# ScalarE writes the first terms of two PSUM accumulations, and one VectorE step finishes each output bank

## The chip, the cores and the metric

One Trainium2 chip, one core of it. The metric is device time in microseconds, from the first to the last instruction of one launch with what lies around it; the kernel's time is the median of its runs. Lower is better. All data are float32 (the adjacency is int32).

## The reference, cut to what matters

`x` is 16 x 512 x 512 (batch, node, feature), one condition vector of 512 per batch, an adjacency with 11 labels, 20 key nodes, 16 heads of 32, and two directions `d`. Biases of the projections are small random numbers.

```python
row_zero = exp_v.sum(-1) == 0
q_exp = jnp.where(row_zero[..., None], 0.0, q[:, None, :])
vcq = jnp.concatenate([exp_v, q_exp], axis=-1)
self_feat = vcq @ W_self.T + b_self
output = self_feat
for d in range(2):
    A = adj_f if d == 0 else jnp.swapaxes(adj_f, 1, 2)
    A = A[:, :, :NONGT, :]
    cond = A.sum(-1)
    vb = A @ w_bias + b_bias
    output = output + _gat_attention(self_feat, cond, vb, Wq[d], bq[d], Wk[d], bk[d], Wout[d], bout[d])
rel = jax.nn.relu(output)
return exp_v + rel
```

`_gat_attention` takes queries from all 512 nodes and keys and values from the first 20, masks scores where `cond` is zero, adds `vb`, takes the softmax over the 20 keys and multiplies by the values and `Wout`.

## The kernel before, in words

Everything is held transposed: feature on the 128 partitions in four chunks, node along the free axis. A setup stage folds `Wq` and the keys into one matrix `g` per batch and `Wout` and the values into `vd`, so that the loop over the 16 batches has three kinds of matmul. Each is issued in pieces of 32 output partitions, four of which run side by side.

**self_feat (`product`, L251).** The product of `x` with half of the weights is done as a 2 x 2 block product with seven block products instead of eight (Strassen's scheme in Winograd's form). `x_sum` (L234, GpSimd) forms the sums of `x` blocks; `weight_sums` did so once for the weights. Products 1, 6, 7 and 4 accumulate in this order in `ps_a` (two banks, one for each half of the rows), and the running sum is read between them; product 2 goes to `ps_d`; products 5 and 3 accumulate in `ps_c`. The term of the condition vector is rank one: the flag row `nz` (is the row of `x` non-zero) times a column `qw`. `partial` (L286, VectorE) adds it while it moves `ps_a` into a block of `sf`, in two instructions; `joined` (L298, VectorE) adds `ps_d` or `ps_c` to a block. `block(b, f, l)` is half `f` of the features by half `l` of the nodes. The first 20 nodes come from the setup by `new_self` (ScalarE).

**scores (L350).** 128 nodes a tile (`nt` 0 to 3), both directions and all heads, into `ps_s`. Then, for each tile: `weigh` (VectorE) adds the mask and bias table `full` (L380), takes the maximum (L384) and subtracts it (L388), `expo` (ScalarE, L393), `normal` (VectorE sum L416 and reciprocal L417, GpSimd multiplication L418) and `turn` (VectorE transposition, L425).

**attend (L427).** For a whole batch: weights times `vd`, 24 matmuls into the four banks `ps_o`, with `start` on the first round. `finish` (L442) adds `sf` (VectorE, L445) and takes bias and ReLU (ScalarE, L447); `residual` (GpSimd, L450) adds `x`; `store` sends the rows on SP's queue.

**masks.** `mask_mul` (ScalarE, 11 instructions, L318) multiplies labels by `w_bias`; `mask_count` (VectorE L323, GpSimd L324) counts edges; `mask_sum` (VectorE, L329) sums; `mask_spread` (ScalarE, 32-partition copies, L338) lays the sum out for the heads; `full_add` (GpSimd, L345) makes `full`. `row_sum` (ScalarE, L193) makes the row sums of `x` two batches ahead.

The order on each engine is the order of the program text; there is no scheduler. Batches overlap: in iteration `b`, tile 0 has product 4, half of the scores, the other half, and product 3, all of batch `b`; tile 1 has scores; tile 2 has the attend block of batch `b-1`, scores, and products 1 and 2 of batch `b+1`; tile 3 has product 6, scores, products 7 and 5 of `b+1`. So on TensorE one batch reads: 4, scores 0, 3, scores 1, attend, scores 2, 1, 2, 6, scores 3, 7, 5. PSUM has two double banks for `ps_s` and four single banks that `ps_a` (0 and 1), `ps_d` (2), `ps_c` (3) and `ps_o` (0 to 3) take in turn. Loads wait in SP's queue, each behind a named instruction (`done[...]`).

Of the kernel before, what the change touches and what calls it, by code (L numbers as in the profile page):

```python
# [13 lines left out]
P = 128  # L14
# [4 lines left out]
def gat_kernel(  # L19
# [55 lines left out]
    qw = const.tile([P, C, B], F32, name="qw")  # L75
    bo = const.tile([P, C], F32, name="bo")
# [174 lines left out]
    def product(b, n):  # L251
# [11 lines left out]
        if n == 1:  # L263
            parts[b, "a"] = [bank(f"ps_a{b}_{i}", i if b else None) for i in range(2)]
        if n == 2:
            parts[b, "d"] = bank(f"ps_d{b}", 2 if b else None)
        if n == 5:
            parts[b, "c"] = bank(f"ps_c{b}", 3 if b else None)
        for i in range(2):
            for k in range(2):  # L270
                for a in range(HL):
# [12 lines left out]
                    nc.tensor.matmul(to, lhs, x[:, k], start=start, stop=stop, skip_group_check=n != 2)  # L284

    def partial(b, f, l):  # L286

        to = block(b, f, l)
        for i in range(2):
# [3 lines left out]
            )  # L293

# [132 lines left out]
    def attend(b, banks, tiles=slice(0, NT), start=True, stop=True):  # L427
# [4 lines left out]
        for first, runs in ((True, ((1, 2, 1), (5, 2, 3))), (False, ((0, 1, 0), (3, 1, 2), (4, 1, 2), (7, 1, 4)))):  # L432
            for at, n, j in runs:
                for a in range(HL):
# [4 lines left out]
                        start=start and first, stop=stop and not first,  # L439
                    )  # L440

    def finish(b, o, banks):  # L442

        for c in range(C):
            done["add", c] = nc.vector.tensor_add(o[:, c], banks[c], sfs[b][:, c])  # L445
        for c in range(C):
            nc.scalar.activation(o[:, c], o[:, c], AF.Relu, bias=bo[:, c : c + 1])  # L447

    def residual(b, c, o):
        nc.gpsimd.tensor_add(o[:, c], o[:, c], xs[b][:, c])  # L450
        outs.append((b, c, o))
# [9 lines left out]
    with tc.tile_pool(name="setup", bufs=1) as sp, tc.tile_pool(name="ps_acc", bufs=4, space=PSUM) as acc["pool"]:  # L461
# [19 lines left out]
        with tc.tile_pool(name="setup_k", bufs=1) as sk:  # L481
# [90 lines left out]
            for fc in range(C):  # L572
# [14 lines left out]
                nc.scalar.activation(kvT[:, fc], kvn[:, fc], AF.Identity, bias=bs_sb[:, fc : fc + 1])  # L587
            weight_sums()
# [221 lines left out]
    with tc.manual_schedule():  # L810
# [10 lines left out]
        for b in range(B):  # L821
# [7 lines left out]
            for nt in range(NT):  # L829
# [13 lines left out]
                if nt == 0:  # L843
# [4 lines left out]
                    else:  # L848
# [5 lines left out]
                        partial(b, 1, 0)  # L854
# [42 lines left out]
                if nt == 1:  # L897
# [13 lines left out]
                    if last:  # L911
                        for c in (0, 1):
                            nc.scalar.activation(biased[:, c], sfs[b][:, c], AF.Identity, bias=bo[:, c : c + 1])
                    s = weigh(b, nt, pair)
# [16 lines left out]
                if nt == 2:  # L931
# [6 lines left out]
                    if b > 0:  # L938
                        banks = [bank(f"ps_o{b - 1}_{q}", q) for q in range(4)]
                        attend(b - 1, banks)  # L940
# [18 lines left out]
                    if more:  # L959
                        product(b + 1, 1)  # L960
                        product(b + 1, 2)
                        new_self(b + 1)
                    s = weigh(b, nt, pair, (lambda: partial(b + 1, 0, 0)) if more else None)
# [7 lines left out]
                    if b > 0:  # L971
                        for c in (0, 1):
                            residual(b - 1, c, o)
                            store()

                if nt == 3 and more:
                    mask_count(b + 1, 0)
                    product(b + 1, 6)
                    joined(b + 1, "d", 0, 0)
# [6 lines left out]
                    partial(b + 1, 0, 1)  # L986
# [125 lines left out]
```

## Time and profile before

| | |
|---|---|
| median of 3 runs | 581.45 us (580.94 to 582.77) |
| span of the profiled execution | 578.9 us, of which the runs' median is 2.55 more |
| mean granted TensorE clock | 0.998 |
| one batch in the middle of the loop | 30.46 us |
| DMA | 123.26 MB, 212 GB/s over the span |

The profile gives no time for the profiled execution other than its span. A profile's busy shares are over the whole span, so they mix the setup with the loop; the prediction reads one batch in the middle (between 305 and 336 us), in which every engine repeats the same rows with the same lengths from batch to batch. In a timeline row the columns are start, length, engine, line, operation, output and inputs, shapes and count; square brackets at its end give the idle time of the engine before it and what ended it.

### The profile page before, as it was taken

The page shows a single profiled execution, that of the slowest core. Times are in us where ns is not written, and L with a number is a line of the kernel's source. Part 1 is how long each engine was busy: PE and PEld are TensorE (multiplying, and loading weights), DVE is VectorE, ACT ScalarE, POOL GpSimd, SP SyncE. Part 2 cuts the span into 40 slices and gives each one's busy share as a digit, 9 for nine tenths or more (in the row PEclk, how much of TensorE's full clock was granted, in tenths as well). Part 3 has the DMA queues.
Part 4 walks back from the last instruction along what each step waited for, and adds up shares of the span by engine and source line. Part 5 has one row for each costly group of instructions (what it writes and reads, how often), then busy time and mean ns, then how long its engine had stood idle before and what let it go on. Part 6 is the DMA issues. An engine that isn't in the chain of part 4 may idle for free.

```text
span 578.9 us, 31006 instructions
## 1 busy us (share of the span) xinstructions
PE 572.2 (99%) x13508; PEld 434.1 (75%) x13508; DVE 492.9 (85%) x790; ACT 393.6 (68%) x1162; POOL 404.6 (70%) x383
## 2 busy tenths in 40 slices
PE   9999999999999999999999999999999999999996
PEld 6544458888878787878778787877887878787873
DVE  0675776979898989898999999898989898989896
ACT  1234554687878777778786868687887877777571
POOL 2726986658586776858585867776858677785874
PEclk9999999999999999999999999999999999999999
DMA  8998997867777767777676777566666766674404
GB/s 315 382 396 283 333 361 233 237 195 219 209 233 185 220 187 204 213 185 228 167 220 166 222 166 220 164 206 180 204 193 192 195 192 189 192 208 111 147 19 147
DMA packets 98788, 123.26 MB, mean 213 GB/s; under 512 B 18877, under 2 KB 66969, under 8 KB 96605
## 3 DMA queue, kind: packets, MB, share of 16 engines
q1 hardware_dynamic: 96268, 117.54, 67.8%
q0 software_dynamic: 1392, 2.43, 1.8%
q8 instruction: 106, 1.74, 1.3%
q10 hardware_dynamic: 992, 1.31, 0.6%
q14 instruction: 30, 0.24, 0.1%
HBM read 82.30 MB, written 40.24 MB: 212 GB/s over the span
## 4 chain that ended last, share of the span: by engine, by line
PE 98%; DVE 1%; issue 0%; DVEq 0%
PE ps_s L366 46%; PE ps_a L284 19%; PE ps_c L284 9%; PE ps_o L436 6%; PE ps_d L284 5%; PE ps_v L658 3%; PE ps_k L598 3%; PE ps_kv L541 1%; PE ps_o L813 1%; PE ps_warm L500 1%; PE ps_nz L214 0%; PE ps_s L355 0%; PE _g(2, 2, 0, 14, 16)0_845 L692 0%; PE _g(0, 2, 0, 14, 16)0_448 L692 0%; PE g(3, 2, 0, 14, 16)0_1055 L692 0%
## 5 line engine op out<-in xcount | busy, mean ns | idle before, releaser
L366 PEld LDWEIGHTS ps_s<-g,sf 128*32 128x32 f32 x8192 | 263.6, 110 | 21.9 <-issue 14.8
L366 PE MATMUL ps_s<-g,sf 128*32 128x152 f32 x8192 | 278.1, 293 | 0.7 <-issue 0.7
L338 ACT COPY both<-add 32x80 f32<-32x80 f32 x512 | 130.9, 256 | 60.9 <-DVE add L329 55.1
L418 POOL TENSOR_TENSOR s<-s,sm 128x640 f32<-128x640 f32 x63 | 80.4, 1275 | 96.8 <-DVE sm L417 52.5
L345 POOL TENSOR_TENSOR full<-cq,both 128x640 f32<-128x640 f32 x64 | 100.3, 1568 | 26.9 <-issue 20.9
L318 ACT ACTIVATE prod<-adj,wb_sb 128x80 f32<-128x80 int32 x330 | 112.4, 432 | 0.0
L393 ACT ACTIVATE s<-s 128x640 f32<-128x640 f32 x63 | 46.5, 738 | 56.0 <-DVE s L388 55.6
L450 POOL TENSOR_TENSOR o<-o,x 128x512 f32<-128x512 f32 x60 | 76.3, 1293 | 0.0
L380 DVE TENSOR_TENSOR full<-ps_s,full 128x608 f32<-128x608 f32 x63 | 48.6, 772 | 22.5 <-PE ps_s L366 19.4
L284 PE MATMUL ps_a<-t,ws_s 128*32 128x246 f32 x1024 | 59.8, 371 | 0.0
L416 DVE TENSOR_REDUCE sm<-s 128x32 f32<-128x640 f32 x63 | 50.8, 807 | 10.5 <-ACT s L393 10.3
L384 DVE TENSOR_REDUCE ps_s<-full 128x32 f32<-128x640 f32 x63 | 52.2, 828 | 2.2
L425 DVE STREAM_TRANSPOSE wt<-s 128x640 f32<-128x640 f32 x63 | 52.8, 838 | 0.6 <-POOL s L418 0.6
L388 DVE TENSOR_TENSOR s<-full,ps_s 128x640 f32<-128x640 f32 x63 | 51.5, 818 | 1.1
L290 DVE SCALAR_TENSOR_TENSOR sf<-nz,qw,ps_a 128x246 f32<-128x246 f32 x128 | 51.5, 443 | 0.1
L284 PEld LDWEIGHTS ps_a<-t,ws_s 128*32 128x32 f32 x1024 | 34.4, 110 | 16.8 <-issue 0.8
L329 DVE TENSOR_REDUCE add<-prod 128x80 f32<-128x960 f32 x32 | 36.8, 1150 | 7.4 <-ACT prod L318 4.0
L447 ACT ACTIVATE o<-o,bo 128x512 f32<-128x512 f32 x60 | 38.3, 713 | 0.6 <-DVE o L445 0.6
L249 POOL TENSOR_TENSOR t<-x,t 128x492 f32<-128x492 f32 x32 | 36.8, 1151 | 1.3
L436 PE MATMUL ps_o<-wt,vd 32*32 32x512 f32 (+5 forms) x816 | 36.9, 578 | 0.0
L249 POOL TENSOR_TENSOR t<-x 128x492 f32<-128x492 f32 x32 | 36.8, 1151 | 0.0
L445 DVE TENSOR_TENSOR o<-ps_o,sf 128x512 f32<-128x512 f32 x60 | 36.7, 668 | 0.0
(225 smaller groups left out, 715.8 us busy)
## 6 DMA issues: line engine op xcount, KB each, us to landing
g<-g_d SPq DMA_DIRECT2D x60, 304.0 KB
g_d<-st SPq DMA_DIRECT2D x16, 1064.0 KB
out_T<-o SPq DMA_DIRECT2D x60, 256.0 KB
xn<-in_xn SPq DMA_DIRECT2D x56, 256.0 KB
x<-in_xT SPq DMA_DIRECT2D x56, 256.0 KB
adj<-in_adj SPq DMA_DIRECT2D x60, 220.0 KB
nz<-nz_d SPq DMA_DIRECT2D x14, 256.0 KB
wk<-in_wkT SPq DMA_DIRECT2D x2, 1024.0 KB
```

What stands on the lines that cost most here:

```text
L249: done["xsum"] = nc.gpsimd.tensor_sub(t, one, two)
L284: nc.tensor.matmul(to, lhs, x[:, k], start=start, stop=stop, skip_group_check=n != 2)
L290: done["partial"] = nc.vector.scalar_tensor_tensor(to[:, i], nzs[b][:, half(l)], qw[:, 2 * f + i, b : b + 1], parts[b, "a"][i][:, :HN], AL ...
L318: nc.scalar.activation(p[:, :, l], a[:, :, l], AF.Identity, scale=wb_sb[:, l : l + 1])
L338: done["spread"] = nc.scalar.copy(adds[b, h][bass.ts(a, R), :, g], add[r].rearrange("p (t m) -> p t m", t=2))
L345: done["full"] = nc.gpsimd.tensor_add(f, cqs[b].unsqueeze(1).to_broadcast(shape), adds[b, nt // 2][:, nt % 2].unsqueeze(2).to_broadcast(sh ...
L366: nc.tensor.matmul(to, sfs[b][:, k, bass.ds(nt * P + (2 * g + j) * R, R)], of, start=(onto is None and k == 0 and (whole or j == 0)), stop ...
L384: nc.vector.tensor_reduce(mx, f, AX.X, ALU.max)
L418: done["normal"] = nc.gpsimd.tensor_mul(s, s, sm.unsqueeze(3).to_broadcast(full))
L425: nc.vector.transpose(wts[b][:, nt], s.rearrange("p a h m -> p (a h m)"))
L436: nc.tensor.matmul(banks[a][bass.ds(at // 2 * DH, n * DH)].rearrange("p (t n) -> p t n", n=32), vd[r, bass.ds(at * DH, n * DH)], wt[r, :, ...
L450: nc.gpsimd.tensor_add(o[:, c], o[:, c], xs[b][:, c])
```

## The change

For batches from 2 on, `ps_a` is one bank for both halves of the rows. Before the products of a batch, ScalarE writes `nz` times a column of `qw` into that bank (`seed_a`), the same with the difference `qwD` of two columns of `qw` into `ps_d` (`seed_d`), and the difference of the two node halves of `nz`, made by GpSimd, times `qw` into `ps_c` (`seed_c`). The products then accumulate onto these with no `start`. Three of the four `partial` steps become one ScalarE copy each (`copied`), the fourth (`lifted`) stays on VectorE. For outputs of batches from 1 on, ScalarE writes `sf` plus bias into the four `ps_o` banks in tile 1 of the iteration (`seed_out`), attend accumulates onto that, and one VectorE instruction per bank takes the maximum with zero and adds `x`. ReLU, residual addition and their places in the order fall away; all four rows of an output are stored at the end of tile 2. Output 0 keeps its ReLU and its GpSimd addition of `x`, the latter now directly behind the former. Batch 0, batch 1's products and the end of the last batch stay as they are.

```diff
+    qwD = const.tile([P, 2, B], F32, name="qwD")
...
+        seeded = b > 1
+        if n == 1 and not seeded:
             parts[b, "a"] = [bank(f"ps_a{b}_{i}", i if b else None) for i in range(2)]
...
+    def seed_a(b):
+        t = bank(f"ps_a{b}", 0)
+        parts[b, "a"] = [t[:, bass.ts(i, HN)] for i in range(2)]
+        parts[b, "w"] = t
+        for i in range(2):
+            nc.scalar.activation(parts[b, "a"][i], nzs[b][:, half(0)], AF.Copy, scale=qw[:, 2 + i, b : b + 1])
+
+    def seed_d(b):
+        t = parts[b, "d"] = bank(f"ps_d{b}", 2)
+        for i in range(2):
+            nc.scalar.activation(t[:, bass.ts(i, HN)], nzs[b][:, half(0)], AF.Copy, scale=qwD[:, i, b : b + 1])
+
+    def seed_c(b):
+        nzD = xsum.tile([P, HN], F32, tag="nzD", name=f"nzD{b}")
+        nc.gpsimd.tensor_sub(nzD, nzs[b][:, half(1)], nzs[b][:, half(0)])
+        t = parts[b, "c"] = bank(f"ps_c{b}", 3)
+        for i in range(2):
+            nc.scalar.activation(t[:, bass.ts(i, HN)], nzD, AF.Copy, scale=qw[:, 2 + i, b : b + 1])
...
+    def summed(b, key, f, l):
+        copied(b, f, l)
+        joined(b, key, f, l)
+
+    def lifted(b):
+        for i in range(2):
+            nc.vector.scalar_tensor_tensor(
+                block(b, 0, 1)[:, i], nzs[b][:, half(1)], qwD[:, i, b : b + 1], parts[b, "a"][i], ALU.mult, ALU.add
+            )
+
+    def copied(b, f, l):
+        nc.scalar.copy(block(b, f, l), flat(b, "w"))
...
         for c in range(C):
-            done["add", c] = nc.vector.tensor_add(o[:, c], banks[c], sfs[b][:, c])
+            if b == 0:
+                done["add", c] = nc.vector.tensor_add(o[:, c], banks[c], sfs[b][:, c])
+                nc.scalar.activation(o[:, c], o[:, c], AF.Relu, bias=bo[:, c : c + 1])
+                nc.gpsimd.tensor_add(o[:, c], o[:, c], xs[b][:, c])
+            else:
+                done["add", c] = nc.vector.scalar_tensor_tensor(
+                    o[:, c], banks[c], 0.0, xs[b][:, c], ALU.max, ALU.add
+                )
+            outs.append((b, c, o))
+
+    def seed_out(b, banks):
         for c in range(C):
-            nc.scalar.activation(o[:, c], o[:, c], AF.Relu, bias=bo[:, c : c + 1])
...
-                        partial(b, 1, 0)
+                        if b > 1:
+                            copied(b, 1, 0)
+                        else:
+                            partial(b, 1, 0)
...
+                    if b > 1:
+                        banks = [bank(f"ps_o{b - 1}_{q}", q) for q in range(4)]
+                        seed_out(b - 1, banks)
                     s = weigh(b, nt, pair)
...
+                        if b > 0:
+                            seed_a(b + 1)
+                            seed_d(b + 1)
                         product(b + 1, 1)
                         product(b + 1, 2)
                         new_self(b + 1)
...
-                    product(b + 1, 6)
-                    joined(b + 1, "d", 0, 0)
+                    else:
+                        summed(b + 1, "d", 0, 0)
+                        product(b + 1, 6)
+                        seed_c(b + 1)
...
-                    partial(b + 1, 0, 1)
+                    else:
+                        lifted(b + 1)
...
+                    if b > 0:
+                        copied(b + 1, 1, 1)
+                    s = weigh(b, nt, pair, (lambda: partial(b + 1, 1, 1)) if b == 0 else None)
```

What this does to the order is seen on ScalarE in two places, and on TensorE in one. In the rows below a line number is that of the kernel they are from; the changed kernel's L332 is `copied`, L295, L300 and L307 are the seeds of `ps_a`, `ps_d` and `ps_c`, L345 `new_self`, L496 `seed_out`, L194 `row_sum`, L357 `mask_mul`, L377 `mask_spread`, L432 `expo`, L405 `scores`, L475 `attend`.

ScalarE from tile 0 to tile 2 of one batch, before (`both` is the spread mask, `prod` the mask products, `s` the softmax, `o` the output):

```order
L338 COPY both_1_6013<-add_1_6011 32x2x40 x8
L393 ACTIVATE s_0_6026<-s_0_6026 128x640
L338 COPY both_1_6013<-add_1_6011 32x2x40 x8
L393 ACTIVATE s_1_6124<-s_1_6124 128x640
L318 ACTIVATE prod_0_6139<-adj_0_6014,wb_sb 128x80 x11
L447 ACTIVATE o_6179<-o_6179,bo 128x512 x4
```

The four ReLUs stand behind the mask products. The same stretch with the change:

```order
L377 COPY both_1_6019<-add_1_6017 32x2x40 x8
L432 ACTIVATE s_0_6032<-s_0_6032 128x640
L377 COPY both_1_6019<-add_1_6017 32x2x40 x8
L496 ACTIVATE ps_o_0_6128<-sf_5104,bo 128x512
L496 ACTIVATE ps_o_1_6129<-sf_5104,bo 128x512
L496 ACTIVATE ps_o_2_6130<-sf_5104,bo 128x512
L496 ACTIVATE ps_o_3_6131<-sf_5104,bo 128x512
L432 ACTIVATE s_1_6138<-s_1_6138 128x640
L357 ACTIVATE prod_0_6153<-adj_0_6020,wb_sb 128x80 x11
L295 ACTIVATE ps_a_6268<-nz_6051,qw 128x246 x2
L300 ACTIVATE ps_d_6271<-nz_6051,qwD 128x246 x2
```

Four writes of the output banks now stand ahead of the `exp` of tile 1, and the four ReLUs have given way to the seeds of `ps_a` and `ps_d`. On TensorE the attend block of that iteration begins so (each row with the semaphores that it waits for; before, no row of this block waits for Activation):

```order
L405 MATMUL ps_s_1_6049<-g_5601,sf_5705 32x152 x63
L475 MATMUL ps_o_0_6128<-wt_5540,vd_6012 64x512 [waits DVE_49,DMAHW2_49,PE_49,Activation_49]
L475 MATMUL ps_o_1_6129<-wt_5540,vd_6012 64x512 [waits DMAHW3_49,Activation_49]
L475 MATMUL ps_o_2_6130<-wt_5540,vd_6012 64x512 [waits DMAHW4_49,Activation_49]
L475 MATMUL ps_o_3_6131<-wt_5540,vd_6012 64x512 [waits DMAHW5_49,Activation_49]
```

It did not move, but each of its first four matmuls now waits for ScalarE. ScalarE from the `exp` of tile 2 to tile 0 of the next iteration, with the change:

```order
L432 ACTIVATE s_2_5709<-s_2_5709 128x640
L332 COPY sf_5705<-ps_a_5667 128x2x246
L307 ACTIVATE ps_c_5744<-nzD_5742,qw 128x246 x2
L194 ACTIVATE xn_0_5547,rs_5750<-xn_0_5547 128x512 x2
L194 ACTIVATE xn_1_5594,rs_5750<-xn_1_5594 128x512 x2
L377 COPY both_0_5763<-add_0_5761 32x2x40 x16
L332 COPY sf_5705<-ps_a_5667 128x2x246
L432 ACTIVATE s_3_5880<-s_3_5880 128x640
L357 ACTIVATE prod_1_5890<-adj_1_5461,wb_sb 128x80 x11
L332 COPY sf_5705<-ps_a_5667 128x2x246
```

The three L332 rows and the L307 row are new here; the rest stood in this order before. Products 6 and 4 and the second half of tile 0's scores wait for the three copies in turn, product 5 for the seeds of `ps_c`.

44 lines of the change are left out of this document (21 added, 23 removed).

## The prediction

> **What bounds the kernel now.** I read first the busy times and the chain that ended last, then the waits of TensorE, then one steady batch in the timeline of each engine.
>
> ```profile
> PE 572.2 (99%) x13508; PEld 434.1 (75%) x13508; DVE 492.9 (85%) x790; ACT 393.6 (68%) x1162; POOL 404.6 (70%) x383
> PE 98%; DVE 1%; issue 0%; DVEq 0%
> ```
>
> The chain of waits is TensorE for 98% of the span, so TensorE ends last almost everywhere. A busy share can hide short waits, so the timeline of one batch has to confirm it (start, length, engine, line; microseconds from the span's start):
>
> ```profile
> 305.58 1.84 PE L284 MATMUL ps_c<-x,ws_s 128*32 128x246 f32 x32
> ...
> 311.48 2.24 PE L436 MATMUL ps_o<-wt,vd 32*64 32x512 f32 x48
> 313.65 4.34 PE L366 MATMUL ps_s<-g,sf 128*32 128x152 f32 x128
> 317.81 1.84 PE L284 MATMUL ps_a<-x,ws_v 128*32 128x246 f32 x32
> ...
> 321.13 1.85 PE L284 MATMUL ps_a<-t,ws_s 128*32 128x246 f32 x32
> 322.80 4.31 PE L366 MATMUL ps_s<-g,sf 128*32 128x152 f32 x128
> 326.93 1.85 PE L284 MATMUL ps_a<-t,ws_s 128*32 128x246 f32 x32
> ...
> 330.26 1.84 PE L284 MATMUL ps_a<-t,ws_v 128*32 128x246 f32 x32
> ```
>
> From start to start a product takes 1.66 us, a tile of scores 4.13 to 4.16, the attend block (L436) 2.17. Seven products, four tiles and one attend make 30.3 to 30.4 us. The batch is cut at two marks: E0 = 305.58, where the scores of tile 0 have ended, and E2 = 317.81, where those of tile 2 have.
>
> ```profile
> 305.58:317.81 12.23, 12.23 (x344) 9.72 (x336) 11.24 (x17) 8.35 (x27) 6.87 (x6) 1.00 0.64 161
> 317.81:336.04 18.23, 18.23 (x456) 14.47 (x449) 16.57 (x28) 15.12 (x45) 15.15 (x14) 1.00 0.74 213
> ```
>
> These windows (columns: length, PE, PEld, DVE, ACT, POOL, granted clock, DMA) show a batch of 30.46 us without a TensorE gap: at most 0.1 us of it is not matmul spacing. VectorE works 27.81, ScalarE 23.47, GpSimd 22.02. So relief of VectorE or GpSimd buys nothing, and each new wait of TensorE is paid in full. ScalarE is idle for 7 us a batch, but in its own places:
>
> ```profile
> 301.04 3.74 ACT L318 ACTIVATE prod<-adj,wb_sb 128x80 f32<-128x80 int32 x11
> ...
> 308.55 0.74 ACT L393 ACTIVATE s<-s 128x640 f32<-128x640 f32 x1 [0.34 <-DVE s L388]
> 309.31 2.12 ACT L338 COPY both<-add 32x80 f32<-32x80 f32 x8
> 314.29 0.74 ACT L393 ACTIVATE s<-s 128x640 f32<-128x640 f32 x1 [2.86 <-DVE s L388]
> ...
> 318.57 2.55 ACT L447 ACTIVATE o<-o,bo 128x512 f32<-128x512 f32 x4
> ...
> 321.52 0.74 ACT L393 ACTIVATE s<-s 128x640 f32<-128x640 f32 x1 [0.25 <-DVE s L388]
> 322.16 0.61 ACT L193 ACTIVATE xn<-xn 128x512 f32<-128x512 f32 x1
> ...
> 324.52 0.18 ACT L193 ACTIVATION_READ_ACCUMULATOR xn<-xn 128x1 f32 x1
> 326.59 4.27 ACT L338 COPY both<-add 32x80 f32<-32x80 f32 x16 [1.88 <-DVE add L329]
> ```
>
> **The change part by part.** Removed per batch: three pairs of VectorE `partial`, four ReLUs on ScalarE, four GpSimd residual additions. By the windows above neither VectorE nor GpSimd is what TensorE waits for, so I cost these at nothing. The four new VectorE finishing steps replace four additions; their cover is the tile of scores behind the attend block (4.16 us from 313.65 to 317.81), in which VectorE needs 3.47 from the additions to L380:
>
> ```profile
> 311.69 0.79 DVE L380 TENSOR_TENSOR full<-ps_s,full 128x608 f32<-128x608 f32 x1 [0.81 <-PE ps_s L366]
> ...
> 314.88 2.45 DVE L445 TENSOR_TENSOR o<-ps_o,sf 128x512 f32<-128x512 f32 x4
> ...
> 318.35 0.73 DVE L380 TENSOR_TENSOR full<-ps_s,full 128x608 f32<-128x608 f32 x1
> ...
> 319.85 0.84 DVE L290 SCALAR_TENSOR_TENSOR sf<-nz,qw,ps_a 128x246 f32<-128x246 f32 x2
> 320.61 0.81 DVE L388 TENSOR_TENSOR s<-full,ps_s 128x640 f32<-128x640 f32 x1
> ...
> 322.10 1.03 DVE L323 TENSOR_REDUCE cond<-adj 128x80 f32<-128x880 int32 x1
> ```
>
> Without that cover they would delay the next softmax by as much as they overrun it. The stores go out earlier on SP's queue, past one key load; the output rows are written by then, so nothing queues behind them.
>
> Added on ScalarE are ten instructions that write PSUM (four of 512, six of 246) and three copies out of PSUM (492). No row has ScalarE writing PSUM. Nearest rows, with GpSimd's small operation:
>
> ```profile
> L318 ACT ACTIVATE prod<-adj,wb_sb 128x80 f32<-128x80 int32 x330 | 112.4, 432 | 0.0
> L587 ACT ACTIVATE kvT<-kvn,bs_sb 128x320 f32<-128x320 f32 x4 | 2.2, 562 | 5.3 <-DMA bs_sb<-in_b_self 3.8 <-DVE kvn L579 1.4
> L555 ACT COPY q<-ps_q 128x512 f32<-128x512 f32 x1 | 0.6, 586 | 9.3 <-PE ps_q L551 9.3
> L324 POOL TENSOR_SCALAR prod<-cond 128x80 f32<-128x80 f32 x32 | 18.2, 569 | 4.5 <-DVE cond L323 1.8
> ```
>
> Four output seeds: as the four ReLUs they replace in count, 2.55 us. A seed of 246 columns lies between 0.43 (80) and 0.56 (320); I take 0.50 and no overlap, since the second of a pair waits for the first. A copy of 492: 0.60, by L555. GpSimd's new subtraction of 246: at least 0.57, at most 1.15 (the L249 row quoted below, 492 columns); I take 0.6.
>
> The first new wait is that of the attend block on TensorE. By the order of instructions shown with the change, the four output seeds stand on ScalarE behind the second half of the mask's spread (L338 at 309.31), and each of the first four attend matmuls waits for the seed of its bank. From the end of a tile's scores to the start of its `exp`: 0.21 (311.48 to 311.69) + 2.60 (311.69 to 314.29) = 2.81. Counted from E0: `exp` at 2.81; spread done 2.88 later (308.55 to 311.43) at 5.69; seeds done at 8.24; signal 0.10 (L388 ends at 321.42, `exp` starts at 321.52), 8.34. TensorE reaches its fourth attend matmul at 5.90 (311.48 - 305.58) + 3 x 0.09 (2.17 for 24) = 6.17. Wait: **2.2 us**. The 2.86 us that ScalarE idles before the next `exp` do hold 2.55 us of seeds, but TensorE wants them when that gap begins, not when it ends. Queued behind this wait are the attend block, the next scores and all later matmuls; on ScalarE the `exp` of tile 1 is not delayed, since its own tile lets it start only at 5.90 + 2.81 = 8.71.
>
> The seeds of `ps_a` and `ps_d` are only just hidden: mask products 9.35 to 13.09, seeds of `ps_a` done at 14.1, while TensorE comes to product 1 at 8.34 + 21 x 0.09 + 4.16 = 14.4. Were ScalarE 0.3 later, product 1 would wait by as much as it is late beyond that.
>
> The second place is ScalarE from the `exp` of tile 2 to the last of the three new copies: product 6 waits for the first copy, product 4 for the second, the second half of tile 0's scores (which reads the rows that it writes) for the third. Counted from E2: `exp` at 2.81, first copy 3.45 to 4.05. Product 6 may start at 4.15; TensorE was there at 3.32 (321.13). Wait 0.8.
>
> Next in ScalarE's queue are the seeds of `ps_c`. They need a GpSimd subtraction that is queued behind GpSimd's part of the mask count:
>
> ```profile
> 323.96 0.56 POOL L324 TENSOR_SCALAR prod<-cond 128x80 f32<-128x80 f32 x1
> 324.61 1.15 POOL L249 TENSOR_TENSOR t<-x,t 128x492 f32<-128x492 f32 x1
> ```
>
> VectorE's count (L323) starts 3.75 us after L380, less 0.76 for the removed pair (319.85 to 320.61): at 3.20, done 4.23. GpSimd: 0.10, 0.65 (323.96 to 324.61), 0.6, 0.10, so the seeds start at 5.68 and end at 6.68. Behind them wait the row sums, 2.54 (322.16 to 324.70): 9.22; the spread, 4.27: 13.49 (the mask sum that it needs is ready at 8.0, since it ended near 8.77, when the spread began, and comes 0.76 earlier); the second copy: 14.09. Product 4 was ready at 4.15 + 1.66 + 4.14 + 3.32 = 13.27 and starts at 14.19. Wait 0.9. Then `exp` 0.64, mask products 3.74, third copy 0.60: 19.07. TensorE, after product 4 and half a tile, stands there at 17.92 and goes on at 19.17. Wait 1.25. Together **3.0 us** a batch, as the start of that half shows, which was at 16.16 (336.04 less half a tile of 2.07, less E2).
>
> Three batches differ. In batch 1 the first output still has its ReLUs and now four GpSimd residuals stand ahead of the normalisation:
>
> ```profile
> 134.67 1.84 PE L284 MATMUL ps_a<-x,ws_v 128*32 128x246 f32 x32
> ...
> 136.18 2.56 ACT L447 ACTIVATE o<-o,bo 128x512 f32<-128x512 f32 x4
> ...
> 136.19 1.28 POOL L418 TENSOR_TENSOR s<-s,sm 128x640 f32<-128x640 f32 x1 [1.47 <-DVE sm L417]
> ...
> 138.94 2.56 POOL L450 TENSOR_TENSOR o<-o,x 128x512 f32<-128x512 f32 x2
> ...
> 556.19 1.33 ACT L913 ACTIVATE biased<-sf,bo 128x512 f32<-128x512 f32 x2
> ```
>
> The normalisation starts about 136.9 + 2 x 2.56 = 142.0 instead of 136.19; the transposition, the mask count and GpSimd's subtraction wait for it, so the seeds of `ps_c` come about 6.1 later: 9.1 instead of 3.0. In batch 15 the L913 pair stands ahead of the output seeds: 2.2 + 1.3 = 3.5. Batch 14 has no row sums, and the mask sum limits instead: 1.8.
>
> Sum: attend 13 x 2.2 + 3.5 = 32.1; the second place 9.1 + 12 x 3.0 + 1.8 = 46.9; together **79 us**. The profiled span of 578.9 becomes 658; the median of the runs, 581.45, lies 2.55 above that span, which gives **660 us**.
>
> Bounds from the rows: with output seeds as short as L555 and 0.1 of overlap, as the ReLUs show it (3 x 0.49 + 0.59 = 2.06 instead of 2.55, 14 times), and seeds of `ps_c` that are never late, so that the mask sum limits (1.2 less, 12 times), 21 us less: 639. With 0.1 more at each of four waits, output seeds without that overlap (0.3 more) and the subtraction at 1.15 (0.55 more), 13 times, 16 to 17 us more: 677.
>
> The Trainium skill ("ScalarE: Activation LUTs", section "Step-by-step: what each stage is for") says that ScalarE writes PSUM faster than SBUF. No row here shows that; by it the sum would lie near the lower of these bounds.
>
> **The rivals.** (1) Only the attend block waits: ScalarE, being ahead after it, meets the later copies. For it: TensorE's lateness gives ScalarE 2.2 us. Against: the `exp` of tile 2 that heads the second place itself waits for TensorE's tile, so the lead is lost there. It gives 32.1 plus 5.0 in batch 1, where the seeds of `ps_a` stand behind the ReLUs (136.18 + 2.45 + 1.0 against 134.67): 619. (2) The clock falls in the waits, and the tile behind each runs slower. The only long pause of TensorE shows how (windows as above):
>
> ```profile
> 574.00:575.00 1.00, 0.20 (x22) 0.00 (x0) 0.97 (x5) 0.00 (x0) 0.00 (x0) 1.00 0.79 280
> ...
> 577.00:578.00 1.00, 0.00 (x0) 0.00 (x0) 0.00 (x0) 0.00 (x0) 0.00 (x0) 0.50 0.33 97
> ```
>
> The last matmul ends near 574.2, and by 577 the clock is at half. A wait of 2.2 us is a little short of that pause, which speaks against; if it fell once a batch for 2.5 us, TensorE would lose 1.25 in 14 batches: 677. The Trainium skill's "TensorE: Matmul & The Clock Gate" (Part 1) halves the clock only after an idle window of about 3.4 us; by that rule it stays up in all but the odd batch. The trace agrees so far that it stayed at 1.00 through the loop. (3) The other side: the output seeds are done when TensorE arrives, because ScalarE's idle 2.86 us take them, and the copies are met too. That needs ScalarE 2.2 us earlier at the attend block, and decides at 311.75, its fourth matmul. TensorE's own sum of 30.35 against 30.46 then leaves up to 1.5 us: 580.
>
> **How the numbers follow.** My forecast 0.72, only the attend wait 0.12, the clock 0.12, seeds hidden 0.04. The likeliest time is 660, its own range 639 to 677. Reaching toward the first two rivals until two tenths are left out: 628 to 682. Faster or slower means more than 0.3% from 581.45, about what this kernel's measurement can tell; only the last rival can be there, half faster, half the same: 0.02, 0.02, slower 0.96.
>
> **What would show it.** Right: TensorE gaps before `ps_o` of about 2 us released by ScalarE, smaller ones before product 6, product 4 and the second half of tile 0's scores; a batch of about 35.6 us; granted clock 1.00. Wrong: a batch near 30.5 (rival 3), gaps before `ps_o` alone (rival 1), a clock below 1.00 in the loop (rival 2), or VectorE as the releaser, which my walk never makes the last.

## The result, and the profile after

| | before | changed kernel |
|---|---|---|
| median of 4 runs | 581.42 us (580.94 to 582.77) | 660.29 us (658.60 to 661.89) |
| ratio of the times | | 1.135 (95% interval 1.132 to 1.138) |
| span of the profiled execution | 578.9 us | 660.1 us |
| mean granted TensorE clock | 0.998 | 0.995 |
| one batch in the middle | 30.47 us | 35.67 us |

The change costs 79 us. The page of the changed kernel, its busy times and its chain that ended last:

```profile
PE 610.4 (92%) x13508; PEld 448.4 (68%) x13508; DVE 473.0 (72%) x707; ACT 450.9 (68%) x1288; POOL 341.4 (52%) x341
ACT 37%; PE 32%; DVE 11%; POOL 10%; issue 8%; DMA 1%; SPq 0%; DVEq 0%; ACTq 0%; POOLq 0%
```

TensorE was 98% of the chain and is now 32%. ScalarE leads it with 37% although it is busy only 68% of the span: it sets the end by when it does things, not by how much it does. The waits of TensorE (what it waited for; total, times, longest):

```profile
PE ps_a L286 <- ACT sf L332: 17.3, 24, 0.8
PE ps_s L405 <- ACT sf L332: 11.4, 14, 0.8
PE ps_a L286 <- ACT ps_a L295: 4.8, 1, 4.8
PE ps_o L475 <- ACT ps_o L496: 4.5, 7, 1.7
```

All four releasers are ScalarE's copies (L332) and seeds (L295, L496). The last row shows far less than the attend block costs, because it counts only the idle time before the first matmul. TensorE's timeline of one batch shows the rest:

```profile
334.50 1.87 PE L286 MATMUL ps_a<-t,ws_v 128*32 128x246 f32 x32 [0.65 <-ACT sf L332]
...
339.26 2.27 PE L405 MATMUL ps_s<-g,sf 128*32 128x152 f32 x64 [0.82 <-ACT sf L332]
341.35 1.84 PE L286 MATMUL ps_c<-x,ws_s 128*32 128x246 f32 x32
...
347.79 4.02 PE L475 MATMUL ps_o<-wt,vd 32*64 32x512 f32 x48 [0.47 <-DMA cq<-cq_d]
351.75 4.34 PE L405 MATMUL ps_s<-g,sf 128*32 128x152 f32 x128
355.90 1.84 PE L286 MATMUL ps_a<-x,ws_v 128*32 128x246 f32 x32
...
360.17 1.87 PE L286 MATMUL ps_a<-t,ws_s 128*32 128x246 f32 x32 [0.76 <-ACT sf L332]
```

E0 is now 341.35 and E2 355.90. Between the start of the attend block and that of the next scores lie 3.96 us; before, 2.17. The block is not slower: its first four matmuls each wait for the seed of their bank. The bracket names a DMA, but each of these four starts 0.05 us after its seed ends: at 347.79, 348.40, 349.01 and 349.62, after seeds that end at 347.74, 348.35, 348.96 and 349.57. ScalarE's rows:

```profile
333.79 0.57 ACT L332 COPY sf<-ps_a 128x492 f32<-128x492 f32 x1
...
338.65 0.56 ACT L332 COPY sf<-ps_a 128x492 f32<-128x492 f32 x1
...
347.05 2.52 ACT L496 ACTIVATE ps_o<-sf,bo 128x512 f32<-128x512 f32 x4
...
354.36 0.95 ACT L295 ACTIVATE ps_a<-nz,qw 128x246 f32<-128x246 f32 x2
...
359.47 0.55 ACT L332 COPY sf<-ps_a 128x492 f32<-128x492 f32 x1
361.82 0.97 ACT L307 ACTIVATE ps_c<-nzD,qw 128x246 f32<-128x246 f32 x2 [1.80 <-POOL nzD L304]
```

The fourth output seed ends at 349.57, 2.1 us after TensorE was ready for its fourth attend matmul (343.01 + 4.16 + 3 x 0.09 = 347.44). Each copy ends 0.05 to 0.15 us before the TensorE row that waits for it: 334.36 before 334.50, 339.21 before 339.26, 360.02 before 360.17. The first seeds of `ps_a` end at 355.31 and just make it to E2.

Batch 1 stands apart. TensorE's row of product 1, and windows of the trace there (length, PE, PEld, DVE, ACT, POOL, granted clock, DMA):

```profile
141.05 3.51 PE L286 MATMUL ps_a<-x,ws_v 128*32 128x246 f32 x32 [4.77 <-ACT ps_a L295]
```

```profile
139.00:141.00 2.00, 0.00 (x0) 0.00 (x0) 0.82 (x1) 1.97 (x5) 2.00 (x3) 1.00 0.46 163
141.00:143.00 2.00, 1.95 (x20) 0.99 (x24) 0.00 (x0) 1.67 (x4) 2.00 (x2) 0.52 0.00 0
143.00:144.00 1.00, 1.00 (x16) 0.47 (x12) 0.00 (x0) 0.00 (x0) 1.00 (x2) 0.50 0.00 0
```

After a wait of 4.77 us the clock is at 0.50, and product 1 takes 3.28 us to the start of product 2 (141.05 to 144.33) instead of 1.66.

Measured between the marks, the 81.2 us that the span grew are: 13 attend blocks x 2.32 (14.55 instead of 12.23) = 30.2; 12 second places x 2.88 (21.12 instead of 18.24) = 34.6; batch 1, 8.0; the second place of batch 14, 1.8; the stretch behind the last E0, 4.9; the stretch up to the first E0, 1.9, which in the kernels below lies between -1.0 and 2.7 without pattern; less 0.2 for one batch of the kernel before that was longer.

### The profile page after: what moved, and what is told of

It reads as the page before. It is cut to its first block, busy times and chain, and to the rows that moved or that the text cites. A ratio compares the mean times of both kernels' runs of the same rounds, so it can differ in the third digit from the quotient of the medians.

```text
span 660.1 us, 31023 instructions
## 1 busy us (share of the span) xinstructions
PE 610.4 (92%) x13508; PEld 448.4 (68%) x13508; DVE 473.0 (72%) x707; ACT 450.9 (68%) x1288; POOL 341.4 (52%) x341
## 4 chain that ended last, share of the span: by engine, by line
ACT 37%; PE 32%; DVE 11%; POOL 10%; issue 8%; DMA 1%; SPq 0%; DVEq 0%; ACTq 0%; POOLq 0%
ACT prod L357 15%; PE ps_s L405 14%; ACT both L377 9%; ACT xn L194 5%; POOL full L384 3%; PE ps_c L286 3%; PE ps_v L704 3%; POOL s L457 3%; PE ps_k L644 3%; DVE ps_s L423 3%; ACT s L432 2%; DVE s L427 2%; DVE full L419 2%; ACT sf L332 2%; ACT ps_c L307 2%
## 5 line engine op out<-in xcount | busy, mean ns | idle before, releaser
L405 PE MATMUL ps_s<-g,sf 128*32 128x152 f32 x8192 | 283.3, 293 | 13.8 <-ACT sf L332 11.4
L405 PEld LDWEIGHTS ps_s<-g,sf 128*32 128x32 f32 x8192 | 263.9, 110 | 40.0 <-issue 18.2
L377 ACT COPY both<-add 32x80 f32<-32x80 f32 x512 | 130.6, 255 | 27.1 <-DVE add L368 21.3
L357 ACT ACTIVATE prod<-adj,wb_sb 128x80 f32<-128x80 int32 x330 | 112.3, 431 | 0.0
L432 ACT ACTIVATE s<-s 128x640 f32<-128x640 f32 x63 | 46.5, 738 | 84.3 <-DVE s L427 84.0
L286 PE MATMUL ps_a<-t,ws_s 128*32 128x246 f32 x1024 | 60.9, 371 | 10.4 <-ACT sf L332 9.9
L475 PE MATMUL ps_o<-wt,vd 32*32 32x512 f32 (+5 forms) x816 | 62.4, 598 | 7.3 <-ACT ps_o L496 4.5
L286 PEld LDWEIGHTS ps_a<-t,ws_s 128*32 128x32 f32 x1024 | 37.6, 110 | 27.2 <-issue 16.8
L489 DVE SCALAR_TENSOR_TENSOR o<-ps_o,x 128x512 f32<-128x512 f32 x56 | 34.8, 684 | 20.0 <-issue 17.9
L475 PEld LDWEIGHTS ps_o<-wt,vd 32*32 32x32 f32 (+1 forms) x816 | 16.1, 113 | 43.5 <-ACT ps_o L496 29.5
L286 PE MATMUL ps_a<-t,ws_v 128*32 128x246 f32 x512 | 30.3, 372 | 7.6 <-ACT sf L332 7.4
L286 PE MATMUL ps_a<-x,ws_v 128*32 128x246 f32 x512 | 31.4, 387 | 4.8 <-ACT ps_a L295 4.8
```

Of the source, the lines that this page charges most:

```text
L286: nc.tensor.matmul(to, lhs, x[:, k], start=start and not seeded, stop=stop, skip_group_check=n != 2 or seeded)
L357: nc.scalar.activation(p[:, :, l], a[:, :, l], AF.Identity, scale=wb_sb[:, l : l + 1])
L377: done["spread"] = nc.scalar.copy(adds[b, h][bass.ts(a, R), :, g], add[r].rearrange("p (t m) -> p t m", t=2))
L405: nc.tensor.matmul(to, sfs[b][:, k, bass.ds(nt * P + (2 * g + j) * R, R)], of, start=(onto is None and k == 0 and (whole or j == 0)), stop ...
L432: done["exp"] = nc.scalar.activation(sw, sw, AF.Exp)
L475: nc.tensor.matmul(banks[a][bass.ds(at // 2 * DH, n * DH)].rearrange("p (t n) -> p t n", n=32), vd[r, bass.ds(at * DH, n * DH)], wt[r, :, ...
```

## The experiments

The question after this result is whether ScalarE's place or its amount of work costs the time. Windows of one batch of the changed kernel, E0 to E2 and E2 to E0:

```profile
341.35:355.90 14.55, 14.09 (x344) 10.23 (x337) 11.58 (x17) 11.86 (x33) 5.24 (x5) 1.00 0.49 130
355.90:377.01 21.11, 18.87 (x457) 15.07 (x449) 14.71 (x20) 15.73 (x49) 12.32 (x12) 1.00 0.65 187
```

ScalarE works 27.59 us a batch, 4.1 more than before, and that would fit into the old 30.46. One can move this work without lessening it. The marks in the table are the starts of product 3 (E0) and product 1 (E2), each for a batch in the middle.

| run | median us | ratio to before (95%) | E0 to E2 | E2 to E0 |
|---|---|---|---|---|
| before | 579.9 to 581.4 | 1 | 12.23 | 18.24 |
| changed kernel | 660.29 | 1.135 (1.132 to 1.138) | 14.55 | 21.12 |
| out_only | 624.55 | 1.075 (1.071 to 1.078) | 14.62 | 18.24 |
| self_only | 677.79 | 1.166 (1.160 to 1.173) | 16.45 | 20.75 to 21.6 |
| seeds_early | 634.99 | 1.093 (1.089 to 1.097) | 14.01 | 19.84 |
| flags_early | 647.14 | 1.114 (1.111 to 1.118) | 14.55 | 20.02 |
| copies_dve | 641.07 | 1.105 (1.101 to 1.108) | 15.20, some 16.5 | 18.75 |
| seeds_two | 633.17 | 1.091 (1.089 to 1.093) | 12.73 | 21.13 |
| first_out | 664.20 | 1.143 (1.139 to 1.148) | 14.55 | 21.12 |
| five | 602.98 | 1.038 (1.036 to 1.041) | 12.80 | 18.24 |
| four_old | 593.26 | 1.021 (1.016 to 1.025) | 12.79 | 18.24 |
| dose_one | 686.68 | 1.181 (1.176 to 1.186) | 15.28 or 16.5 to 16.9 | 21.13 |
| dose_two | 699.23 | 1.202 (1.196 to 1.209) | 17.0 to 18.4 | 21.13 |

**Each part alone.** out_only keeps the output part and gives the products back their old start, which overwrites some of what the output seeds wrote; every instruction is there:

```diff
-        seeded = b > 1
+        seeded = False
...
-                            copied(b, 1, 0)
+                            partial(b, 1, 0)
...
-                            seed_a(b + 1)
-                            seed_d(b + 1)
```

> Only the output part: self_feat is computed as before, and ScalarE writes self_feat plus bias into the four output banks, with one VectorE maximum-and-add at the end. (The products start their banks as before, so some columns of the output seeds are overwritten by the first attend matmul instead of added to; every instruction is there.) Place theory (TensorE waits where ScalarE's queue is late): attend waits 2.3 us in 13 batches and 3.6 in the last, nothing else: 614 us. Load theory (time follows what ScalarE has to do in all): the four seeds replace four ReLUs of the same length, so about 581.

```profile
329.98 4.03 PE L475 MATMUL ps_o<-wt,vd 32*64 32x512 f32 x48 [0.53 <-ACT ps_o L496]
```

The attend wait stands alone, E2 to E0 is as before. Here the bracket names ScalarE's seed, where the changed kernel's named a DMA for the same gap. The 10 us over the expected 614 are mainly in batch 1, where GpSimd's additions for output 0, now ahead of the normalisation, stretch E2 to E0 from 18.36 to 23.38, and the last batch.

self_only keeps the seeds and copies of the products and finishes the output as before (ReLU on ScalarE, addition on GpSimd at their old places).

> Only the self_feat part: seeds of ps_a, ps_d and ps_c, copies on ScalarE; the output is finished as before with addition, ReLU and residual. Place theory: attend does not wait; product 1 waits some 4.3 us, since the seeds of ps_a stand behind mask products and ReLUs; the queue behind GpSimd's residuals makes the seeds of ps_c late; a batch of about 35.2 us and 647 us in all, so that the two parts alone cost more together (33 + 66) than the change (79). Load theory: all the added ScalarE work is here, so 660.

TensorE's product 1, ScalarE ahead of it, and windows there:

```profile
364.17 3.51 PE L286 MATMUL ps_a<-x,ws_v 128*32 128x246 f32 x32 [4.03 <-ACT ps_a L295]
```

```profile
360.72 2.54 ACT L486 ACTIVATE o<-o,bo 128x512 f32<-128x512 f32 x4
363.17 0.95 ACT L295 ACTIVATE ps_a<-nz,qw 128x246 f32<-128x246 f32 x2
```

```profile
360.10:364.17 4.07, 0.04 (x5) 0.01 (x1) 3.97 (x7) 4.04 (x10) 3.45 (x3) 0.79 0.68 195
364.17:365.50 1.33, 1.33 (x16) 0.69 (x20) 0.48 (x1) 1.30 (x4) 1.33 (x2) 0.50 0.71 159
...
367.50:369.00 1.50, 1.50 (x20) 0.74 (x16) 0.00 (x0) 1.23 (x3) 0.90 (x1) 0.50 0.07 27
369.00:371.00 2.00, 2.00 (x40) 1.16 (x36) 0.67 (x2) 2.00 (x8) 0.00 (x0) 0.93 0.64 164
```

The wait was expected, its consequence was not: late in it or just behind it the clock falls to half, for 3.4 or 6.8 us. In this batch products 1 and 2 last 3.28 and 2.56 us instead of 1.66 each; over the loop they lose 1.7 us in eight batches, 2.4 to 2.5 in five and nothing in one, 26 us together, most of the 31 between 647 and 677.79. Apart, the two parts cost 43 and 97 us, and together only 79: with the output part the ReLUs no longer stand ahead of the seeds of `ps_a`, and the attend wait gives ScalarE the time to write them. The products' part alone makes TensorE wait too, but mostly at another place: of the 20.75 us from E2 to E0, 18.24 are as before and 1.7 are the slow clock, so the second place costs 0.8 here and 2.9 in the changed kernel.

**The same work at other places.** seeds_early writes three output seeds in tile 0, behind the third copy:

```diff
                             copied(b, 1, 0)
+                            banks = [bank(f"ps_o{b - 1}_{q}", q) for q in range(3)]
+                            seed_out(b - 1, banks, range(3))
...
-                        seed_out(b - 1, banks)
+                        seed_out(b - 1, banks, range(3, 4))
```

> The change, with three of the four output seeds moved on ScalarE from tile 1 to tile 0, behind the third copy and ahead of the mask's spread, into banks that are free by then; the same instructions. Place theory: attend waits 0.4 us instead of 2.3, product 1 now waits some 1.3 (it comes earlier than its seeds) and product 6 no longer; ScalarE's chain from the exp of tile 2 on starts 1.8 earlier in each batch: 635 us. Load theory: the same work, 660.

```profile
337.72 2.74 PE L475 MATMUL ps_o<-wt,vd 32*64 32x512 f32 x48
340.38 4.34 PE L405 MATMUL ps_s<-g,sf 128*32 128x152 f32 x128
345.82 1.87 PE L286 MATMUL ps_a<-x,ws_v 128*32 128x246 f32 x32 [1.09 <-ACT ps_a L295]
```

ScalarE does exactly as much as in the changed kernel, and 25 us are gone. The attend block lasts 2.66, half a microsecond over its 2.17, and 1.1 us come back before product 1: the seeds that were only just hidden behind the attend wait are now late.

flags_early moves GpSimd's subtraction for the seeds of `ps_c` ahead of the mask count.

```diff
+                        if b > 0:
+                            flag_step(b + 1)
                     store()
...
-        nc.gpsimd.tensor_sub(nzD, nzs[b][:, half(1)], nzs[b][:, half(0)])
+        nzD = nzDs[b]
```

> The change, with GpSimd's subtraction for the seeds of ps_c moved ahead of its part of the mask count. Place theory: ScalarE does not wait for GpSimd before these seeds (1.8 us a batch in the profile), the spread then starts when the mask sum is ready, 1.1 us earlier: 12 to 13 batches, 646 us. Load theory: the same work, 660.

```profile
352.25 0.98 ACT L311 ACTIVATE ps_c<-nzD,qw 128x246 f32<-128x246 f32 x2
```

The row has lost its 1.80 us bracket. E2 to E0 falls by 1.1, as the lower bound of the prediction had it (1.2 where the mask sum limits). The two runs reject the theory that ScalarE's load alone decides: it expected 660 of both.

seeds_two adds to seeds_early that the seeds of `ps_a` and `ps_d` go ahead of the mask products.

```diff
                             seed_d(b + 1)
+                            mask_mul(b + 1, 0)
                         product(b + 1, 1)
```

> The run with three output seeds in tile 0 (634.99) had a new wait of 1.09 us before product 1, on the seeds of ps_a, which stand behind the mask products. Here the seeds of ps_a and ps_d also go ahead of the mask products. Theory A (place in ScalarE's queue alone): the seeds of ps_a can end 1 us before TensorE arrives, the mask products end when the exp of tile 2 is ready, so the 1.09 goes: 34.0 - 1.1 = 32.8 us a batch, 617 to 624. Rival B (total of ScalarE's work: the wait turns up again before product 6 or product 4, behind the mask products): 632 to 637.

```profile
346.61 1.87 PE L286 MATMUL ps_a<-t,ws_s 128*32 128x246 f32 x32 [0.99 <-ACT sf L332]
```

Theory A missed here, and rival B had the time and the place right: the wait before product 1 went (12.73), but E2 to E0 rose from 19.84 to 21.13, and the batch stayed at 33.85. ScalarE's total is not the limit, though: it is busy 27.71 of these 33.85 us. The wait before product 1 had been a lead: the softmax of tile 2 runs from the end of its scores while TensorE stands, so its `exp` (1.64 us after E2 in seeds_early) and the first copy were in time. Without the wait the `exp` starts 3.17 after E2, right behind the mask products, and both are late again. A wait removed on TensorE buys nothing while the chain `exp`, copy, seeds, row sums, spread, copy behind the scores of tile 2 is longer than TensorE's work beside it.

copies_dve breaks that chain: the three copies go back to VectorE, where `partial` stood.

```diff
-        nc.scalar.copy(block(b, f, l), flat(b, "w"))
+        nc.vector.tensor_copy(block(b, f, l), flat(b, "w"))
```

> The three ScalarE copies of the changed kernel go back to VectorE, to the places of the old partial steps; all seeds stay. The second place cost 2.9 us a batch, all of it before instructions that wait for a copy. Theory A (each wait of TensorE is an instruction of ScalarE that stands late in its queue): product 6, product 4 and the second half of tile 0's scores no longer wait, E2 to E0 falls from 21.1 to 18.2-18.8 us, the attend wait of 2.3 us stays; 13 x 2.3 + batch 1 (8) + last batch: 620 to 630. Rival B (the seeds of ps_c, late behind GpSimd's subtraction, push the mask's spread and with it the softmax of tile 3, and TensorE meets that chain anyway): E2 to E0 stays at 20 or more, 645 to 655. Rival C (VectorE, with copies and finishing steps, becomes the bound): VectorE named as the releaser of TensorE in every batch.

```profile
341.48 4.02 PE L474 MATMUL ps_o<-wt,vd 32*64 32x512 f32 x48 [1.12 <-ACT ps_o L495]
```

E2 to E0 is 18.75, so all but 0.5 of the second place was the copies. What is left is a wait of up to 0.3 us on VectorE's third copy, ahead of the second half of tile 0's scores, in twelve batches. But 641 is over the expected 620 to 630. The attend wait grew from 2.32 to 2.97, since TensorE is back at E0 sooner while the spread that holds up ScalarE's output seeds still starts when the late mask sum lets it; and in three of the twelve batches with this wait E0 to E2 was 1.3 to 1.5 longer still, taken up below. The copies' work leaves ScalarE together with their place in its queue (26.09 us busy a batch instead of 27.59), so this run does not part place from amount, as seeds_early and flags_early do.

five makes all moves at once (copies, output seeds, flags, seeds of `ps_a` and `ps_d`), with first_out's edit. first_out alone changes only the first output, whose ReLU and addition run on VectorE:

```diff
-                nc.scalar.activation(o[:, c], o[:, c], AF.Relu, bias=bo[:, c : c + 1])
-                nc.gpsimd.tensor_add(o[:, c], o[:, c], xs[b][:, c])
+                nc.vector.tensor_scalar(o[:, c], o[:, c], bo[:, c : c + 1], 0.0, ALU.add, ALU.max)
+                nc.vector.tensor_add(o[:, c], o[:, c], xs[b][:, c])
```

> Only the first output differs from the changed kernel: its ReLU with bias and its addition of x run on VectorE, right behind its first addition, so that ScalarE's seeds of batch 2 and GpSimd's normalisation no longer stand behind them. Theory A (in batch 1 the seeds of ps_a wait behind the ReLUs, TensorE waits 4.8 us and the clock halves for a few us): the 4.8 us wait goes, and with it the slow product 1; batch 1 takes about 36 us instead of 39.4, VectorE's four to eight extra steps cost up to 2 of it: 655 to 659. Rival B (batch 1 is late for another reason): no change, 660.

> All moves together: copies back on VectorE, three output seeds in tile 0, GpSimd's subtraction ahead of the mask count, seeds of ps_a and ps_d ahead of the mask products, first output finished by VectorE. ScalarE still writes all ten seeds of a batch, so it still does 2.85 us more than before less nothing but the copies. Theory A (place decides): no wait of TensorE in the loop is longer than 0.3 us, batch 30.5 to 30.9 us; 582 to 592. It cannot be below 580, since TensorE's own sum is 30.35 a batch. Rival B (work that ScalarE took on cannot be placed without some wait, or VectorE becomes the bound): 32 us a batch or more, over 603.

VectorE in batch 1 of first_out:

```profile
133.88 0.65 DVE L485 TENSOR_TENSOR o<-ps_o,sf 128x512 f32<-128x512 f32 x1
134.57 1.82 DVE L486 TENSOR_SCALAR o<-o,bo 128x512 f32<-128x512 f32 x1
...
142.59 0.82 DVE L455 TENSOR_REDUCE sm<-s 128x32 f32<-128x640 f32 x1
```

The expectation of 655 to 659 was missed, the run took 664.20: VectorE's twelve steps hold up the softmax sum from 133.88 to 142.59, and what E0 to E2 won in batch 1 (15.81 instead of 17.25) E2 to E0 lost (26.29 instead of 21.91). five has this batch too, so its 603 does not decide; its batches, at 31.04, lie just above theory A's 30.9 and well below rival B's 32. four_old is five with the first output finished as in the kernel before:

> The run with all moves together (602.98), but the first output is finished as in the kernel before: ReLU on ScalarE, additions of x on GpSimd at their old places. That run's batch 1 took 39.0 us (31.04 in the others), because VectorE's twelve steps for output 0 lasted 8.7 us and held up the softmax of tile 1. Theory A (that one-off is VectorE's queue): batch 1 falls to 32 to 35 us, 596 to 600; batches unchanged at 31.0 (an attend wait of 0.55, for the fourth output seed). Rival B (ReLUs of ScalarE ahead of the seeds of ps_a cost as much): 602 to 604. Neither can bring it below 590, since 13 waits of 0.55 and the last batch's 4 us stay.

Windows of a batch in the middle of four_old, E0 to E2 and E2 to E0:

```profile
309.52:322.30 12.78, 12.78 (x344) 9.88 (x336) 11.63 (x18) 9.45 (x28) 6.64 (x6) 1.00 0.56 157
322.30:340.54 18.24, 18.24 (x456) 14.48 (x449) 16.14 (x24) 16.76 (x52) 11.02 (x11) 1.00 0.72 212
```

Batch 1 is 32.76, and the time is 593.26, below the 596 to 600 of theory A. All ten seeds are still ScalarE's (26.21 us busy a batch), E2 to E0 is free of waits, and one attend wait of 0.55 is left, for the fourth output seed. What remains over before is that (13 x 0.55 = 7 us), batch 1 (1.6) and the end (2.9). Even this arrangement gains nothing, since TensorE does the same matmuls: VectorE's 27.77 a batch is what it was (27.81), and GpSimd's relief, 17.66 instead of 22.02, was not waited for.

**How the clock answers to a wait.** dose_one and dose_two are the changed kernel with the output seeds of the first one or two banks written twice, so that all seeds come later and nothing else changes.

```diff
+                        seed_out(b - 1, banks[:1])
                         seed_out(b - 1, banks)
```

> The changed kernel, with the output seed of the first bank written twice, so that ScalarE is 0.63 us later with all four seeds and TensorE's wait at the attend block grows from 2.3 to 2.9 us. Theory A (the wait is ScalarE's lateness and costs what it lasts): 14 x 0.63 = 9 us more, 669. Theory B (waits near 3 us make the granted clock fall to 0.50 behind them, as in the run with the copies back on VectorE, where 5 of the 13 batches with a wait of 2.9 us lost another 1.4 us): in some batches 1.4 us more, 672 to 688, and a mean clock under 0.99.

> The same with the first two banks written twice: ScalarE 1.26 us later, the attend wait 3.6 us. Theory A (the wait costs what it lasts): 14 x 1.26 = 18 us more, 678. Theory B (waits over about 3 us halve the clock for 3 to 5 us): another 1.4 to 2.2 us in every batch, 695 to 710, and the granted clock at 0.50 in the window behind each wait. Neither: ScalarE does as much in the loop as TensorE's batch has room for, so a plain load theory gives no change, 660.

Two batches of dose_one with the same attend wait, behind that wait; first one at 15.28:

```profile
318.00:319.50 1.50, 1.50 (x6) 0.37 (x4) 1.47 (x3) 1.49 (x3) 1.50 (x3) 1.00 0.70 158
319.50:321.00 1.50, 1.50 (x28) 0.47 (x42) 0.42 (x1) 1.48 (x4) 1.43 (x1) 1.00 0.61 171
```

then one at 16.81:

```profile
356.00:357.50 1.50, 1.50 (x11) 0.17 (x10) 0.32 (x1) 1.50 (x4) 1.33 (x1) 0.63 0.70 177
357.50:359.00 1.50, 1.50 (x37) 0.28 (x32) 0.00 (x0) 1.50 (x6) 0.00 (x0) 0.50 0.35 119
```

and dose_two:

```profile
405.00:406.50 1.50, 1.50 (x13) 0.37 (x12) 0.45 (x1) 1.48 (x3) 1.46 (x1) 0.77 0.63 180
406.50:408.00 1.50, 1.50 (x26) 0.28 (x32) 0.00 (x0) 1.50 (x6) 0.00 (x0) 0.50 0.40 143
```

PE reads as busy throughout (its ends are modelled); the granted clock and the matmul counts tell the two apart. A wait of 2.3 us (changed kernel) leaves E0 to E2 at 14.55 to 14.57 in all 13 batches and the clock at 1.00; 3.05 us (dose_one) halves it in 9 of 13, at 1.2 to 1.6 us each; about 3.8 us (dose_two, 14.55 + 2 x 0.73 - 12.23) in all 13, at 1.0 to 2.4 each, and 4.2 (self_only) in 13 of 14. copies_dve, with 2.97, lost it in three of twelve (dose_one's expectation says five of 13, which was a miscount). So a microsecond more of waiting cost two to three: 9 us of added seeds became 26 in dose_one, 18 became 39 in dose_two.

## Why the prediction was right

The forecast was 660 and the time 660.29. The mechanism held, but so close a hit is luck: single terms were off by up to 1.6 us either way, and the first E0 came 1.9 later, for which there was no term. Its steps, as they were put:

- **TensorE's batch has no gap, so each new wait is paid in full, and relief of VectorE or GpSimd buys nothing**: right. The matmuls kept their durations at full clock, and in four_old GpSimd's relief by 4.4 us a batch is worth nothing. No run relieves VectorE without new waits, so for VectorE it stays an argument from the batch without gaps.
- **The attend wait, 2.2 us**: 2.32 measured. Seeds of 2.55 were 2.52, and they end 8.22 after E0, where the working had 8.24. Four ReLUs into SBUF in batch 1 of the changed kernel lasted 2.54, so the Trainium skill's note that ScalarE writes PSUM faster ("ScalarE: Activation LUTs", "Step-by-step: what each stage is for") is hardly to be seen here: 2.52 against 2.54.
- **The second place, 3.0 us**: 2.88 measured. Product 6 starts 4.27 after E2 (working: 4.15), the seeds of `ps_c` at 5.92 (5.68), and, in the batch before, whose E2 is 320.24, product 4 at 14.26 (14.19) and the second half of tile 0's scores at 19.02 (19.17). That GpSimd's subtraction delays the seeds is shown by flags_early, that the copies are what TensorE meets by copies_dve.
- **Seeds of `ps_a` only just hidden**: right, by 0.6 us; seeds_early and self_only show what happens when they are not.
- **Batch 1, 9.1 us in its second place**: 8.0 measured, but by another way. 4.5 of them come before E2: the seeds of `ps_a` stand behind the ReLUs, which I had named under the first rival and left out of the forecast. The other 3.5 are behind E2, where the halved clock of product 1 alone takes 1.6. GpSimd was late as forecast (its normalisation starts at 143.28, working: 142.0), but by then TensorE was late too, so the seeds of `ps_c` come 6.7 after E2 and not 11.8. Also, from 136.19 to 142.0 are 5.8 us, where the working has 6.1. The sum hit by luck.
- **Batch 14, 1.8**: 1.8. **The last attend, 3.5**: the fourth attend matmul starts 3.3 late (635.22; without a wait 625.71 + 6.18 = 631.89). The stretch behind the last E0 grew by 4.9 all the same, since the clock was at 0.50 from 636.0 to 639.4: the rest of the attend block lost 1.2 and the scores behind it 0.5 (638.36 to 643.13, 4.77 instead of 4.27).
- **Rival 2, the clock**: rightly left out of the sum for waits of 2.2 us, behind which it stayed at 1.00 in all 13 batches. It did fall behind the two longer waits, in batch 1 and at the last attend, and cost some 3.3 us there, which the sum had at nothing. The Trainium skill's idle window of about 3.4 us ("TensorE: Matmul & The Clock Gate", Part 1) is longer than dose_one's wait of 3.05 us, in which TensorE moreover ran its first attend matmuls, and yet nine of 13 batches lost the clock; the last section comes back to it.
- **Rivals 1 and 3**: the first is refuted by the changed kernel's own waits before L286 and L405 on `sf`, the third by the attend block. seeds_two shows the grain of truth in the first: a wait of TensorE does give ScalarE a lead, for the next chain that begins ahead of the wait.

## What to carry to other kernels

Giving a half-idle engine more work costs by where that work stands in its queue: walk the queue from the event that heads it to each instruction that the bounding engine waits for, and price the lateness there. When one wait is taken away, look for the chain that it gave time to; here three of the moves (seeds_early, seeds_two, copies_dve) brought part of the wait back at the next place. Where only the place is changed, with the same work, this is shown for the output seeds and for the seeds of `ps_c`; for the copies place and amount went together. And keep waits of TensorE short: in the middle batches here 2.3 and 2.4 us kept the clock, 2.97 us lost it in three of twelve and 3.8 us in all 13, and each loss added 1.0 to 2.5 us.

## What the runs showed of the hardware that was not expected

The clock's fall at 3 us is not a sharp edge. With the same wait of 3.05 us, nine batches of dose_one lost the clock and four did not, and one batch of self_only kept it through 4.2 us. The clock records of the traces show what the length leaves out. Every stretch at 0.50 but the last of a run lasts 3.41 or 6.83 us, and within a run all begin on one grid with steps of 3.413 us. In dose_one they begin at 243.74, 281.28, 356.38 and 393.92, which are 11, 22 and 11 steps apart. One step of this grid ahead of a fall, the fall, and the step behind it (windows as above):

```profile
353.00:356.40 3.40, 2.28 (x11) 0.78 (x16) 3.19 (x4) 3.34 (x6) 3.40 (x4) 1.00 0.44 118
356.40:359.80 3.40, 3.40 (x51) 0.58 (x44) 0.07 (x1) 3.40 (x11) 0.93 (x1) 0.50 0.37 105
359.80:363.20 3.40, 3.40 (x112) 3.40 (x108) 3.37 (x6) 2.51 (x7) 0.00 (x0) 1.00 0.25 70
```

So it matters how a wait lies on this grid, and not its length alone. In batch 1 of seeds_two a wait of 2.5 us (140.31 to 142.84) lay almost wholly in one step (from 140.4), and the clock was at 0.50 in the next. In dose_two, where each batch lost the clock, E0 to E2 repeats 17.35, 17.0 and 18.35 over three batches: these last 116.1 us, which are 34 steps, so the waits meet the grid in the same places again. This agrees with the free-running window of the Trainium skill ("TensorE: Matmul & The Clock Gate", Part 1). But the step ahead of a fall need not be idle, and how empty it must be stays open: one with 16 matmul starts (from 240.1 in the changed kernel) kept the clock, and one with 30 (from 361.4 in dose_two) lost it.

The first VectorE `tensor_scalar` of first_out's four in batch 1 took 1.82 us and the next three 0.48 to 0.49, on equal operands; five shows the same (1.83, then 0.48 to 0.49). In both runs the long one lies beside a GpSimd instruction (`full`, 134.53 to 136.11 in first_out, 135.67 to 137.26 in five) and ends 0.28 us after it, and beside the other three GpSimd does nothing. That points at GpSimd as what it waits for; no run tests it.
